# Cross-attention on one core: running sums of a pair's projection in PSUM tiles of their own, and two pieces of GpSimd's work moved

## The chip, the cores and the metric

One core of one Trainium2 chip runs the kernel. The metric is the device time of one execution in microseconds (us), from runs that are repeated; the profile is of one more execution. TensorE (PE) does the matrix products, with its weight loads in rows of their own (PEld); VectorE (DVE), ScalarE (ACT) and GpSimd (POOL) do the elementwise work; SyncE (SP) issues most transfers. Products land in PSUM, which TensorE writes and VectorE and ScalarE read.

## What is computed

Sixteen batch elements, each with 100 tokens of width 640 (`x`) and 722 context rows of width 384, eight heads of width 80. The last 4 context rows (`ca`) are apart from the first 718 (`enc`). Cut to what matters:

```python
query = x @ Wq
hs = mha(query, enc @ Wk, enc @ Wv)
ca_q1 = einsum('btc,th->bch', ca, Wq_ca)[:, indices, :]
ca_hs1 = mha(ca_q1, x, x)                      # first stage of the tokens
ca_hs2 = mha(ca_hs1 @ Wq, ca @ Wk_ca, ca @ Wv_ca)
out = (hs + ca_hs2) @ Wout + b_out + x
```

All of it is float32. `mha` is softmax attention over eight heads.

## The kernel before, in words

**Order of the work.** After a set-up, a loop over the 16 batch elements b issues everything in an order written out by hand: `tc.manual_schedule` keeps each engine's instructions in the order in which the program calls them. The framework only adds the waits between engines. An instruction that must wait therefore holds up all that stands behind it on its engine.

**One batch element.** TensorE computes the scores of b (`scores`, L650, in three groups, two of them in two-bank PSUM tiles and one in single banks), then the small products of the tokens' stages (L851, L789), then the values of b and the keys of b + 1 (`Values`, L475, and `Keys`, L506), both from sums of blocks that save products; the last third of the keys (`last_keys`, L600); in odd b the queries of the next two elements (`queries`, L576); then, in some b, the projection of two row tiles of the output (below); then the softmax's row sums (L1540) and the weighted values (L1558). ScalarE and VectorE move results out of PSUM between these; VectorE finds and subtracts maxima (L1382, L713 to L743, L1370), ScalarE takes exponentials (L1378).

**PSUM.** There are eight banks in three pools: `ps2` with two tiles of two banks each (`pair`), `psk` with two single banks (`psumk`) and `ps1` with two single banks (`psum1`). Each pool hands out its buffers in turn, so a tile can be written only when the last reader of the tile two allocations before it in its pool is done. `Keys` A and B and one score group use `psk`; `Values` A and B, the other scores and the last keys use `ps2`; `queries` alternate between `psk` and `ps1`.

**Projection in pairs.** The output's 1600 rows are cut into row tiles r of 128 rows (the last three apart). `ENDS[r]` is the batch element in which tile r's last row lies. Tiles 0 to 9 are projected two at a time (`project_pair`, L1104 to L1168) with a scheme that needs seven products of half-width blocks where a plain one needs eight: the sums of row blocks come from GpSimd (`row_sums`, L1102), those of weights stand ready. Four PSUM banks take part. y is a running sum: a product is added to it, VectorE adds it into the output tile, the next product is added on top, and so on, four times. z is a running sum read twice, v and w are each read once. Before, y and z are the two banks of one `ps2` tile (named `o_ps` in the profile), v and w are single banks (`o_psv`, `o_psw`). The ten tiles make five pairs, in the loop passes b = 3, 6, 8, 11 and 13. In b = 6 and 8 the helper `step` slips VectorE's steps of the next element's first-stage maximum between the adds. The end of the method sets rows of `most`, in which the row sums of the pair were kept, back on GpSimd (L1167).

**Residual and bias.** The output tile `xn` of a row tile is loaded from `x` (`Last.load`, L995, two buffers), GpSimd adds the bias (`add_bias`, L1005), and the projection is added in place (`add` in `project_pair`, L1138). `O_AFTER[r]` says with which element's `Last` this is done; the loop pass is one later. Before, it is one element earlier for the even tile of a pair (passes 2, 5, 7, 10 and 12) than for the odd one. SyncE issues the stores of a finished pair (`store`), the loads of x and the load of the tokens' matrix m (`load_m`) behind VectorE's last running maximum of the scores, in this order.

**GpSimd's queue in a pass** (b from 1 to 13): the first stage's scores of b + 1 (`scores1`, L824, L831); the tokens' keys of b + 2 (`keys`, five small products, L761, read by the next pass's L789); the second stage's probabilities (`softmax3`, L890), for which VectorE has taken sums; then, behind VectorE's second subtraction, `place` (L1067, L1070), the row sums, the bias, `values2` (L927, L931), the memset and the next context's block sums (`enc_sums`, L541). VectorE transposes the probabilities (`spread2`, L900) and stands waiting for them; behind that transpose on its queue are PSUM adds and the subtractions.

Of the kernel before, what the change touches and what calls it, by code (L numbers as in the profile page):

```python
# [14 lines left out]
B, S, H = 16, 100, 640  # L15
# [20 lines left out]
ENDS = [(lo + n - 1) // S for lo, n in OC]  # L36
# [1 line left out]


NPAIRS = 5  # L40
O_AFTER = [ENDS[r | 1] - (r + 1) % 2 for r in range(2 * NPAIRS)] + ENDS[2 * NPAIRS :]
PAIRED = {ENDS[r + 1]: (r, r + 1) for r in range(0, 2 * NPAIRS, 2)}
HT = NH * T

# [114 lines left out]
def kernel(  # L159
# [33 lines left out]
    def pair(name):  # L193
        tile = ps2.tile([P, 2, 512], F32, tag="ps2", name=name)
        return tile
# [4 lines left out]
    def psumk(name):  # L200
        return psk.tile([P, 512], F32, tag="psk", name=name)
# [543 lines left out]
    def load_m(b, behind=None):  # L745
        if b < 2:
            return lambda c: m_sb[c][:, b * HT : (b + 1) * HT]
        mb = small.tile([P, HC, HT], F32, tag="mb", name=f"mb_{b}")
        loaded = nc.sync.dma_start(
            out=mb, in_=m_d[:, :, b * HT : (b + 1) * HT].rearrange("c p n -> p c n")  # L750
        )
        if behind:
            wait_for(loaded, behind)
        return lambda c: mb[:, c]

    def keys(m):

        for c, (_, groups) in enumerate(GROUPS):
            at = [i for i, h in enumerate(groups) if h >= 0]
            n, step = len(at), at[1] - at[0]  # L760
            nc.gpsimd.tensor_tensor(  # L761
                m2[:, c, at[0] : at[-1] + 1 : step, :],
                m(c).unsqueeze(1).to_broadcast([P, n, HT]),
                hmask[:, c, :n].unsqueeze(2).to_broadcast([P, n, HT]),
                ALU.mult,
            )
# [210 lines left out]
    class Last:  # L977
# [6 lines left out]
        def load(self, behind=None):  # L984

            self.xn = {}
            for r, (lo, n) in enumerate(OC):
                if self.b != O_AFTER[r]:
                    continue
# [114 lines left out]
        def project_pair(self, steps):  # L1104

            r0, r1 = PAIRED[self.b]
            t0, t1 = hsTs[r0], hsTs[r1]
            x0, x1 = (xns[r].rearrange("p (k d) -> p k d", k=2) for r in (r0, r1))
            b11, t3 = w_there[0]
            b21, b22 = w_there[1]  # L1110
            tt1, tt2, tt4 = (wout_t[:, i] for i in range(3))
            both = pair(f"o_ps_{r0}")
            y, z = both[:, 0], both[:, 1]
            v, w = psumk(f"o_psv_{r0}"), psumk(f"o_psw_{r0}")

            def product(bank, rows, weights, first=False, last=False):
                for c in range(2):
                    nc.tensor.matmul(  # L1118
                        bank[:, : H // 2],
                        rows[:, c],  # L1120
                        weights[:, c],
                        start=(first and c == 0),
                        stop=(last and c == 1),
                        skip_group_check=True,
                    )

            def rest(bank, rows, k, last=True):
                nc.tensor.matmul(
                    bank[:, : H // 2],
                    rows[:, HC - 1],  # L1130
                    wout_sb[:, HC - 1, k * (H // 2) : (k + 1) * (H // 2)],
                    start=False,
                    stop=last,
                    skip_group_check=True,
                )

            def add(to, left):
                nc.vector.tensor_tensor(to, left, to, ALU.add)  # L1138

            def step(n=1):  # L1140
                if steps:
                    steps(n)

            step()
            product(y, t0[:, :2], b11, True)
            product(z, t1[:, :2], t3, True)
            add(x0[:, 0], y[:, : H // 2])
            step()
            product(y, self.s2, tt2)
            add(x1, both[:, :, : H // 2])  # L1150
            step()
            product(v, t0[:, 2:4], b21, True)
            rest(v, t0, 0)
            product(y, self.s1, tt1)
            add(x0[:, 1], y[:, : H // 2])
            step()
            product(z, t1[:, 2:4], tt4)
            rest(z, t1, 0)
            add(x1[:, 0], z[:, : H // 2])
            step(8)  # L1160
            product(w, self.s4, b22, True)
            rest(w, t0, 1)
            rest(y, t1, 1)
            add(x0[:, 0], v[:, : H // 2])
            add(x0[:, 1], w[:, : H // 2])
            add(x1[:, 1], y[:, : H // 2])
            nc.gpsimd.memset(most[96:, :], LOW)  # L1167
            held.extend((r, xns[r]) for r in (r0, r1))  # L1168
# [183 lines left out]
    for b in range(B):  # L1352
# [24 lines left out]
        def exponential(i):  # L1377
            nc.scalar.activation(st[i], st[i], AF.Exp, scale=SCALE)  # L1378
# [28 lines left out]
        if b == 0:  # L1407
            second.scores1()
            m_next = load_m(b + 2)
            kk.go(3)  # L1410
            top.go(3)
            first_values(3, e_in, (act, act), get=bank)
            top.go(1)
            first_values(0, e_in, (act, act), (0, 1), bank)
            second_next, enc_next = loads()
            enc_next = load_rest(b + 2, enc_next)
            now.scores2()
            kk.go(2)
            top.go()
            kk.go(3)  # L1420
            now.softmax3()
            kk.go(3)
            now.spread2()
            subtract(0)
            exponential(0)
            kk.go(2)
            subtract(1)
            kk.go(3)
            exponential(1)
            subtract(2)  # L1430
            exponential(2)
            last_keys(b + 1, enc)
            keys(m_next)
            enc_sums(enc_next)
            now.values2()
        elif b + 1 < B:
            vv = Values(b, e_in)

            def both(n):
                vv.go(n)  # L1440
                kk.go(n)

            second.scores1(seen)
            store(seen)
            last.load(seen)
            if b == B - 2:
                again()
            if b + 2 < B:
                m_next = load_m(b + 2, seen)
                keys(m_next)  # L1450
            if b == 1:
                load_outputs(nc.sync.dma_start, wout_sb, wout)
            top.go(3)
            both(3)
            now.scores2()
            top.go(1)
            both(2)
            top.go()
            both(2)
            now.softmax3()  # L1460
            both(1)
            now.spread2()
            vv.go(2)
            kk.go(1)
            subtract(0)
            exponential(0)
            vv.go(1)
            last.place(subtract(1))
            if last.b in PAIRED:
                last.row_sums()  # L1470
            last.add_bias()
            now.values2()
            vv.go(1)
            kk.go(2)
            exponential(1)
            vv.go(1)
            kk.go(2)
            both(1)
            both(1)
            if b == 1:  # L1480
                for f in list(wv_there):
                    nc.scalar.copy(wv_sb[:, W_AT[f]], wv_there.pop(f))
            if b == 1:
                nc.gpsimd.dma_start(out=bias, in_=bout[0].partition_broadcast(P))
            second_next, enc_next = loads()
            subtract(2)
            exponential(2)
            last_keys(b + 1, enc)
            if b + 2 < B:
                enc_next = load_rest(b + 2, enc_next)  # L1490
        else:
            vv = Values(b, e_in)
            last.place()
            last.load()
            mine.load()
            last.add_bias(seen)
            top.go(3)
            vv.go(3)
            last.project_few(len(OC) - 2)
            last.project((0,), True, put=False)  # L1500
            top.go(1)
            now.scores2()
            top.go()
            now.softmax3()
            less = subtract(0)
            now.spread2()
            exponential(0)
            wait_for(subtract(2, nc.gpsimd), less)
            now.values2()
            mine.add_bias()  # L1510
            vv.go(5)
            last.put()
            vv.go(1)
            subtract(1)
            exponential(2)
            vv.go(1)
            exponential(1)
            vv.go(5)
# [109 lines left out]
```

## Time and profile before

| | |
|---|---|
| median of 3 runs | 939.08 us (938.87 to 940.33) |
| the profiled execution's own time | 939.93 us |
| its span | 938.2 us |
| instructions | 26084 |
| granted TensorE clock | full in all 40 slices |
| transferred | 69.50 MB, mean 74 GB/s |
| busiest engine after TensorE | VectorE, 660.2 us |

The profile is of one execution. The span runs from its first to its last instruction; what lies around it is the difference to its own time. Rows of a timeline give the start within the span, the duration, engine, line, operation, output and inputs, the shape, how many instructions are put together, and in brackets the idle time of the engine just before them with what ended it. A float32 product of 128 rows is two matmul instructions in the trace for each one in the program. Rows of waits give total, number and longest.

### The profile page before, as it was taken

What the parts mean: (1) busy time and instruction counts of PE and PEld (TensorE: products, weight loads), DVE (VectorE), ACT (ScalarE), POOL (GpSimd) and SP (SyncE); (2) the same over time, 40 slices, a digit from 0 to 9 for tenths busy, and PEclk for the clock granted to TensorE, in tenths of its full rate; (3) what the DMA queues carried; (4) which work ended last, traced back from release to release, by engine and by line L of the source; (5) the groups of instructions that cost most, each with busy time, mean ns of one, the idle gap of its engine ahead of it and who ended that gap; (6) DMA issues with size and microseconds to landing.
All of it is one profiled execution on the core that took longest, in us unless ns stands there. A gap on an engine that the chain in (4) does not pass through costs nothing.

```text
span 938.2 us, 26084 instructions
## 1 busy us (share of the span) xinstructions
PE 921.5 (98%) x11163; PEld 777.7 (83%) x11163; DVE 660.2 (70%) x1116; ACT 374.8 (40%) x649; POOL 611.8 (65%) x646
## 2 busy tenths in 40 slices
PE   9999999999999999999999999999999999999998
PEld 6997879797887979878798787988887888878865
DVE  3358895979739796675957759578792887828784
ACT  1234544444325443432434334344541444414451
POOL 5848857587746868475684746756974578745553
PEclk9999999999999999999999999999999999999999
DMA  8613352050401403140231402204140150401312
GB/s 260 201 45 101 62 120 65 19 140 19 107 12 47 126 21 107 29 129 12 68 88 29 129 12 73 76 21 131 28 108 10 48 137 22 108 11 45 79 50 70
DMA packets 68956, 69.50 MB, mean 74 GB/s; under 512 B 26088, under 2 KB 62632, under 8 KB 68840
## 3 DMA queue, kind: packets, MB, share of 16 engines
q1 hardware_dynamic: 67512, 66.51, 26.8%
q8 instruction: 88, 1.44, 0.7%
q10 hardware_dynamic: 864, 0.98, 0.4%
q0 software_dynamic: 464, 0.34, 0.2%
q14 instruction: 28, 0.23, 0.1%
HBM read 62.14 MB, written 8.94 MB: 76 GB/s over the span
## 4 chain that ended last, share of the span: by engine, by line
PE 91%; DVE 6%; ACT 1%; issue 1%; POOL 0%; DVEq 0%; POOLq 0%; ACTq 0%
PE s_ps L650 12%; PE v_psA L475 10%; PE v_psB L475 8%; PE kT_ps L600 8%; PE a_ps L1558 7%; PE q_ps L576 7%; PE k_psA L506 7%; PE k_psB L506 6%; PE r_ps L1540 4%; PE v_psC L475 3%; PE o_ps L1118 3%; PE k_psC L506 3%; PE y_ps L789 2%; PE v_ps L416 2%; DVE most L1382 2%; PE v_psD L475 1%
## 5 line engine op out<-in xcount | busy, mean ns | idle before, releaser
L824 POOL TENSOR_TENSOR e<-ca,g 100x800 f32<-100x800 f32 x64 | 99.2, 1560 | 105.7 <-DVE most L1382 90.4
L541 POOL TENSOR_TENSOR enc<-enc 128x240 f32<-128x240 f32 x135 | 109.8, 823 | 19.7 <-ACT qp L584 10.1
L475 PE MATMUL v_psA<-wv_sb,enc 128*120 128x320 f32 x352 | 109.6, 434 | 0.4 <-ACT st L678 0.3
L650 PE MATMUL s_ps<-qp,kT 32*120 32x100 f32 x3072 | 97.7, 263 | 0.0
L650 PEld LDWEIGHTS s_ps<-qp,kT 32*120 32x120 f32 x3072 | 94.9, 179 | 2.1 <-issue 0.2
L831 POOL TENSOR_TENSOR e<-e,e 100x800 f32<-100x800 f32 x48 | 90.3, 1882 | 3.8
L475 PE MATMUL v_psB<-wv_sb,enc 128*120 128x320 f32 x296 | 91.8, 433 | 0.0
L506 PE MATMUL k_psA<-enc,wk_sb 128*128 128x240 f32 x360 | 87.8, 367 | 0.6 <-DVE kT L446 0.5
L1370 DVE TENSOR_TENSOR st<-st,over 120x1600 f32<-120x1600 f32 x47 | 86.2, 1834 | 0.0
L1382 DVE TENSOR_TENSOR most<-most,st 120x800 f32<-120x800 f32 x64 | 69.6, 1088 | 21.8 <-ACT st L672 20.7
L506 PEld LDWEIGHTS k_psA<-enc,wk_sb 128*128 128x128 f32 x360 | 68.2, 190 | 17.7 <-DVE kT L446 0.9
L475 PEld LDWEIGHTS v_psA<-wv_sb,enc 128*120 128x120 f32 x352 | 63.2, 183 | 23.2 <-DVE vs L446 1.0
L1378 ACT ACTIVATE st<-st 120x1600 f32<-120x1600 f32 x48 | 73.9, 1540 | 9.1 <-DVE st L1370 8.8
L1393 DVE TENSOR_TENSOR most<-st 120x800 f32<-120x800 f32 x16 | 18.6, 1160 | 81.6 <-ACT st L678 81.6
L506 PE MATMUL k_psB<-enc,wk_sb 128*128 128x240 f32 x300 | 73.1, 366 | 0.1
L475 PEld LDWEIGHTS v_psB<-wv_sb,enc 128*120 128x120 f32 x296 | 54.1, 183 | 21.9 <-DVE vs L446 0.4
L1067 POOL TENSOR_TENSOR hsT<-hsT,ratio 128x500 f32<-128x500 f32 (+22 forms) x26 | 20.5, 789 | 78.3 <-DVE st L1370 73.5
L1558 PE MATMUL a_ps<-st,vs 120*64 120x100 f32 (+1 forms) x1536 | 69.5, 250 | 0.0
L576 PE MATMUL q_ps<-xT,wq_sb 128*128 128x200 f32 x400 | 69.1, 333 | 0.0
L1558 PEld LDWEIGHTS a_ps<-st,vs 120*64 120x64 f32 (+1 forms) x1536 | 66.4, 137 | 2.7 <-issue 2.7
L576 PEld LDWEIGHTS q_ps<-xT,wq_sb 128*128 128x128 f32 x400 | 67.9, 190 | 0.2
L678 ACT COPY st<-s_ps 120x800 f32<-120x800 f32 x64 | 49.7, 829 | 43.9 <-PE s_ps L650 43.9
(193 smaller groups left out, 1906.7 us busy)
## 6 DMA issues: line engine op xcount, KB each, us to landing
pb<-p_d SPq DMA_DIRECT2D x32, 400.0 KB
enc<-in_enct SPq DMA_DIRECT2D x30, 240.0 KB
enc<-in_enct SPq DMA_DIRECT2D x15, 360.0 KB
xT<-in_xt SPq DMA_DIRECT2D x8, 500.0 KB
rest<-in_enct SPq DMA_DIRECT2D x31, 120.0 KB
xn<-in_x SPq DMA_DIRECT2D x11, 320.0 KB
wide_d<-p_d SPq DMA_DIRECT2D x16, 200.0 KB
pb<-wide_d SPq DMA_DIRECT2D x16, 200.0 KB
```

The costliest lines, as they stand in the source:

```text
L475: nc.tensor.matmul(at[0][j][:KN, : H // 2], a_form(self.enc, f)[:, j * KN : (j + 1) * KN], wv_there.get(f, wv_sb[:, W_AT[f]]), start=first ...
L506: nc.tensor.matmul(at[:, i * KT : (i + 1) * KT], wk_sb[:, W_AT[f], i], a_form(self.enc, f), start=(first and i == 0), stop=last, skip_grou ...
L541: nc.gpsimd.tensor_tensor(out, left, right, op)
L576: nc.tensor.matmul(q_ps[:, : 2 * S].rearrange("p (j s) -> p j s", j=2), wq_sb[:, c, n * P : (n + 1) * P], xT[:, :, c, :], start=(c == 0), ...
L600: nc.tensor.matmul(bank[:, i * KT : (i + 1) * KT], weights[c], a_raw(enc, u, c), start=(i == 0 and c == 0), stop=(c == CC - 1), skip_group ...
L650: nc.tensor.matmul(s_ps[bank][:n, 256 * a + lo : 256 * a + lo + rhs.shape[-1]], kT[rows, c, u, j * KN : (j + 1) * KN], rhs, start=bank not ...
L824: first = nc.gpsimd.tensor_tensor(to, self.ca[:, t, :].unsqueeze(1).to_broadcast([S, NH, S]), g[:, :, t].unsqueeze(2).to_broadcast([S, NH, ...
L831: nc.gpsimd.tensor_tensor(e, e, to, ALU.add)
L1370: return engine.tensor_tensor(st[i], st[i], top.over[:KN].unsqueeze(1).to_broadcast([KN, 2, ROWS]), ALU.subtract,)
L1378: nc.scalar.activation(st[i], st[i], AF.Exp, scale=SCALE)
L1382: most_now = nc.vector.tensor_tensor(most[:KN], most[:KN], st[i][:, u], ALU.max)
L1558: nc.tensor.matmul(wides[64 * e : 64 * e + 64, h // 2], slot(i, h, FIRST[e], 64), st[i // 2][: KEYS[i], i % 2, h * S : (h + 1) * S], start ...
```

## The change

Three edits, of which the first two touch the projected pairs and the third every pass from 1 to 13:

- y and z become two single-bank tiles (`o_psy`, `o_psz`) and v and w the two banks of one `ps2` tile (`o_ps`). The add that read y and z in one instruction is split in two; the adds of v and w become one.
- `O_AFTER` of the even tile of a pair becomes that of the odd one: both residual tiles are loaded and get their bias in the pair's own pass.
- `keys` for b + 2 is called behind `softmax3`, not ahead of it; its load stays where it was.

```diff
-O_AFTER = [ENDS[r | 1] - (r + 1) % 2 for r in range(2 * NPAIRS)] + ENDS[2 * NPAIRS :]
+O_AFTER = [ENDS[r | 1] for r in range(2 * NPAIRS)] + ENDS[2 * NPAIRS :]
...
+            y, z = psumk(f"o_psy_{r0}"), psumk(f"o_psz_{r0}")
             both = pair(f"o_ps_{r0}")
-            y, z = both[:, 0], both[:, 1]
-            v, w = psumk(f"o_psv_{r0}"), psumk(f"o_psw_{r0}")
+            v, w = both[:, 0], both[:, 1]
...
             product(y, self.s2, tt2)
-            add(x1, both[:, :, : H // 2])
+            add(x1[:, 0], y[:, : H // 2])
+            add(x1[:, 1], z[:, : H // 2])
...
-            add(x0[:, 0], v[:, : H // 2])
-            add(x0[:, 1], w[:, : H // 2])
+            add(x0, both[:, :, : H // 2])
             add(x1[:, 1], y[:, : H // 2])
...
                 m_next = load_m(b + 2, seen)
-                keys(m_next)
...
             now.softmax3()
+            if b + 2 < B:
+                keys(m_next)
             both(1)
             now.spread2()
```

## The prediction, made before the run

> **What bounds the kernel now.** I read the page's busy times and chain first, then the waits of TensorE alone, then the timeline around a pair's projection.
>
> From the page of before, the busy row of every engine and the chain that ended last:
>
> ```profile
> PE 921.5 (98%) x11163; PEld 777.7 (83%) x11163; DVE 660.2 (70%) x1116; ACT 374.8 (40%) x649; POOL 611.8 (65%) x646
> ...
> PE 91%; DVE 6%; ACT 1%; issue 1%; POOL 0%; DVEq 0%; POOLq 0%; ACTq 0%
> ```
>
> TensorE is busy 921.5 us of a span of 938.2, so it idles 938.2 - 921.5 = 16.7 us. No edit that leaves its matmuls alone can win more than about that, and only edits that touch those idle times win anything. Who causes them (columns: us in total, times, longest):
>
> ```profile
> PE o_ps L1118 <- DVE xn L1138: 6.7, 10, 0.8
> PE k_psE L506 <- DVE vs L446: 1.5, 3, 0.8
> PE z_ps L851 <- issue: 1.4, 2, 0.9
> ```
>
> The first row is the pair projection: ten waits, two in each of five pairs, all for VectorE's adds out of PSUM. It is the largest single wait of the engine that bounds the kernel. One pair in full, batch 3 (start, us, engine, line, out, count, wait in brackets), TensorE and then VectorE:
>
> ```profile
> 255.24 2.32 PE L1118 MATMUL o_ps<-wout_sb,hsT 128*128 128x320 f32 x8
> 258.23 1.31 PE L1118 MATMUL o_ps<-wout_t,most 128*128 128x320 f32 x4 [0.68 <-DVE xn L1138]
> 259.38 1.24 PE L1118 MATMUL o_psv<-wout_sb,hsT 128*128 128x320 f32 x4
> 260.46 0.70 PE L1128 MATMUL o_psv<-wout_sb,hsT 128*128 128x320 f32 x2
> 261.00 1.24 PE L1118 MATMUL o_ps<-wout_t,most 128*128 128x320 f32 x4
> 262.82 1.34 PE L1118 MATMUL o_ps<-wout_t,hsT 128*128 128x320 f32 x4 [0.58 <-DVE xn L1138]
> ...
> 266.16 0.70 PE L1128 MATMUL o_ps<-wout_sb,hsT 128*128 128x320 f32 x2
> ```
>
> ```profile
> 257.60 0.49 DVE L1138 TENSOR_TENSOR xn<-o_ps,xn 128x320 f32<-128x320 f32 x1 [5.60 <-PE o_ps L1118]
> 259.66 0.83 DVE L1138 TENSOR_TENSOR xn<-o_ps,xn 128x640 f32<-128x640 f32 x1 [1.57 <-PE o_ps L1118]
> 262.28 0.49 DVE L1138 TENSOR_TENSOR xn<-o_ps,xn 128x320 f32<-128x320 f32 x1 [1.80 <-PE o_ps L1118]
> ```
>
> The eight matmuls at 255.24 are y's four and z's four. The first add needs y alone, yet begins at 257.60, just behind the end of both (255.24 + 2.32 = 257.56). At 262.82 TensorE wants z and waits for the add at 262.28, which reads y. So y and z, two banks of one tile, are guarded as one thing. That is what the change takes apart.
>
> **The change part by part.**
>
> *Size of what goes.* From 259.38 to 261.00 six matmuls are issued without a wait: 1.62 / 6 = 0.27 us each. From 255.24 to 266.16 there are 34 starts, so 34 x 0.27 = 9.18 us undisturbed against 10.92: the pair loses 1.74 us, of which the brackets show 0.68 + 0.58 = 1.26. The rest, 0.48, is the array emptying before each wait and refilling behind it. Over five pairs: 6.7 from the wait row, plus 5 x 0.48 = 2.4, is **9.1 us**.
>
> *What is late next, first wait.* Take y's start as zero. y ends at 1.24 (the length of four matmuls, as at 259.38); VectorE's add can run from 1.28 to 1.77 (0.04 behind the end, as 257.60 behind 257.56; then 0.49). TensorE resumed 0.14 behind the add (258.23 behind 258.09), so y is free again at 1.91. Meanwhile z's four matmuls keep TensorE until 8 x 0.27 = 2.16. Slack 0.25 us: the wait is covered. The slack is thin. Were the wait just touched, the pair would pay the refill behind it, which four matmuls show as 1.31 against 1.24: I bound what stays at 0 to 0.1 us a pair, and take 0, since the slack is over three times that.
>
> *Second wait.* The next y product starts at 2.16 and ends at 3.40; its add runs from 3.44 to 3.93. TensorE has v's six matmuls from 3.24 to 4.86 before it needs y. Slack 0.8. z then needs only the add of its own bank, which comes from 3.93 to 4.42, and z is wanted at 5.94. In batches 6 and 8 VectorE also works through a maximum between these adds. Batch 6 now:
>
> ```profile
> 421.28 0.98 DVE L715 TENSOR_REDUCE quad<-turned 128x25 f32<-128x800 f32 x1
> 422.93 0.82 DVE L1138 TENSOR_TENSOR xn<-o_ps,xn 128x640 f32<-128x640 f32 x1 [0.68 <-PE o_ps L1118]
> 423.67 0.70 DVE L718 TENSOR_REDUCE side<-quad 32x25 f32<-32x25 f32 x4
> 424.41 1.31 DVE L725 TENSOR_REDUCE mx<-side 32x25 f32<-32x100 f32 x4
> 425.75 0.49 DVE L1138 TENSOR_TENSOR xn<-o_ps,xn 128x320 f32<-128x320 f32 x1
> 426.30 1.34 PE L1118 MATMUL o_ps<-wout_t,hsT 128*128 128x320 f32 x4 [0.78 <-DVE xn L1138]
> ```
>
> The 0.98 us reduction would end near 1.77 + 0.98 = 2.75, ahead of 3.44; the 2.0 us group delays only the third add, whose bank y isn't written again until the last product. So both batches lose their waits too.
>
> *Adds.* One add of 0.83 becomes two of 0.49, and two of 0.49 become one of 0.83: 0.3 us more, then less, on an engine with 278 us idle. Cost 0.
>
> *Where the new tiles wait at their start.* y and z now take the two single-bank buffers that query projections or the next keys had; v and w take the two-bank buffer later than y and z did, so they have more room. In batches 3 and 11 z takes the buffer of the query product before the last, which is copied out a whole product earlier; in 6 and 8 y and z take those of the next keys, with the last third of those keys still ahead of the pair on TensorE. In batch 13 z takes the buffer of the last query product, which ScalarE empties in
>
> ```profile
> 822.48 0.74 ACT L588 ACTIVATE qz<-q_ps,qmask 128x200 f32<-128x200 f32 x2 [1.37 <-PE q_ps L576]
> ```
>
> that is until 823.22, where y starts at 822.28 in before and z is due 1.08 later, at 823.36. A wait of 0 to 0.1 us, once. I take 0.
>
> *Tokens' keys behind the probabilities, 13 batches.* GpSimd and VectorE in batch 3:
>
> ```profile
> 229.86 1.40 POOL L761 TENSOR_TENSOR m<-mb,hmask 128x64 f32<-128x64 f32 x5
> 231.22 0.23 POOL L890 TENSOR_TENSOR p_in<-e,sm 100x32 f32<-100x32 f32 x1
> 236.47 0.78 POOL L1067 TENSOR_TENSOR hsT<-hsT,ratio 128x280 f32<-128x280 f32 x1 [5.02 <-DVE st L1370]
> ```
>
> ```profile
> 231.49 0.21 DVE L900 STREAM_TRANSPOSE p2t<-p_in 128x32 f32<-128x32 f32 x1 [0.17 <-POOL p_in L890]
> 231.63 1.78 DVE L1370 TENSOR_TENSOR st<-st,over 120x1600 f32<-120x1600 f32 x1
> ...
> 242.03 2.10 DVE L1370 TENSOR_TENSOR st<-st,over 120x1600 f32<-120x1600 f32 x1
> ```
>
> The five keys' products (1.40 us) move into the 5.02 us in which GpSimd waits anyway, and the transpose no longer waits 0.17. It stands before VectorE's subtractions and PSUM adds, so up to 13 x 0.17 = 2.2 us come off VectorE's queue. TensorE has no wait row behind that place, so the gain is 0, at most some tenths. The keys are read only by the next batch's first-stage product. What they may cost: they now touch VectorE's subtraction. The row at 242.03 took 2.10 us beside GpSimd's bias add, 1.78 to 1.81 elsewhere, so 0.3 us a batch at most, 13 x 0.3 = 3.9 us of VectorE in the worst case. The Trainium skill ("SBUF — State Buffer", section "Who interferes with whom") speaks against the move: a VectorE instruction with two SBUF inputs contends with a GpSimd instruction that reads SBUF. The trace agrees with it in the 2.10. By that rule the sum would lose those 0.3 us a batch only if TensorE waited for VectorE there; by the rows it doesn't, and the sum stays.
>
> *The even tile's load and bias, one batch later.* In each pair's batch SyncE issues two loads of x, and GpSimd adds two biases. Batch 6:
>
> ```profile
> 414.13 3.14 POOL L1005 TENSOR_TENSOR xn<-xn,bias 128x640 f32<-128x640 f32 x1
> L1005 POOL TENSOR_TENSOR xn<-xn,bias x13: 858/1544/3137, 191.2 to 901.9; 128x640 f32<-128x640 f32 x11, 64x320 f32<-64x320 f32 x2
> 429.38 0.76 POOL L1167 MEMSET most<- 32x800 f32 x1 [4.21 <-PE o_psw L1118]
> ```
>
> The second bias runs from 417.27 and takes 1.54 (the median) to 3.14: done by 418.8 to 420.4. The pair starts at 418.52, and the add that needs this tile is due 3.44 later, at 421.96: slack 1.6 to 3.1 us. Behind it on GpSimd stand values2 and the memset, which idles 4.21 us; the wait for w comes 1.9 earlier, so 2.3 of it is left, against 1.54 to 3.14. At the worst the row sums of the next context start as late as now. In batches 2, 5, 7, 10 and 12 GpSimd is freed by the same amount. The load itself: slices of 0.35 us from 386 us on, in which the issues at 388.9 (320 KB of x, 80 KB of m) run:
>
> ```profile
> GB/s 0 0 0 0 0 0 0 0 0 0 0 110 102 358 348 211 41 0 0 0 0 0 0 0 0 0 0 0 0 0 0 0 23 0 0 0 0 0 0 47
> ```
>
> All has landed by 392. A second 320 KB adds 1 to 1.5 us, some 20 us ahead of 414. The m load behind it has until the keys. Cost 0.
>
> *Sum.* -9.1 us (bounds: 5 x 0.1 + 0.1 = 0.6 for what may stay of the waits; -0.5 for VectorE's earlier transposes, an estimate). The profiled execution took 939.93 us, 1.73 more than its span; it would become 930.8. Its time lies 0.85 above the median of the three runs, 939.08, and against this median the forecast is 939.08 - 9.1 = **930.0 us**.
>
> **The rivals.**
>
> 1. *Half is given back.* TensorE reaches the next batch 1.8 us earlier and may meet an engine that isn't ready, or the first, thin cover fails and only the second wait goes (5 x 0.9 = 4.5). For: the 0.25 us slack. Against: behind scores, VectorE and GpSimd wait for TensorE's results, as the 4.21 us shows. About 934.6 us.
>
> 2. *The waits stay.* If the guards count TensorE's matmuls in order and the first add still goes behind z, nothing moves. For: the add at 257.60 starts with z's end, which fits either reading. Against: 262.82 waits for an add that read y only, which order on TensorE doesn't explain. 939 us.
>
> 3. *Slower: the second bias comes too late.* VectorE's add into the odd tile waits for it, y's next product for the add, TensorE for both. GpSimd's place is 1.6 us of slack (batch 6, at 3.14 us); from there each us costs five, and beyond 1.6 + 1.8 = 3.4 us late the kernel is slower. Five us late would be (5 - 1.6) x 5 - 9.1 = +7.9: 947 us. Against: the transfers are done 20 us before, and GpSimd's queue up to the second bias holds only what it held.
>
> **How the numbers follow.** A measurement can tell about 0.2%, 1.9 us, from no change. Full gain, 929.0 to 931.0: 0.72. More, down to 928.4, if earlier transposes also spare k_psE's 1.5 us: 0.05. Rival 1, 931 to 936: 0.13. Rival 2, within 0.2%: 0.06. Rival 3: 0.04. So faster 0.90, same 0.06, slower 0.04. The range 928.8 to 932.6 holds the full gain, most of the case below it and the near part of rival 1, about 0.8.
>
> **What would show it.** Right: the ten waits of the o_ps row gone or under 0.1 us each; the first add of a pair beginning about 1.3 us behind the pair's first matmul, not 2.36; from the pair's first matmul to the start of its last two, 9.2 us instead of 10.9; the p_in wait of the transpose gone, the k_psE row as it was. Wrong: a wait of TensorE for the new z at its first product; VectorE's add waiting for a bias; a longer subtraction with a TensorE wait behind it; or the pairs shorter by 1.8 us each and the batches between them longer by as much.

## The result, and the profile after

The changed kernel takes 931.04 us (median of 4 runs, 929.79 to 932.29) where the kernel before took 939.37 in the same measurement: ratio 0.991, 95% interval 0.9893 to 0.9927. Measured once more beside other kernels it took 930.76 against 940.05. The forecast was 930.0. The profiled execution took 930.72 us with a span of 929.0, so the span shrank by 938.2 - 929.0 = 9.2 us; the sum had said 9.1.

The page after, busy times and chain:

```profile
PE 918.7 (99%) x11163; PEld 778.2 (84%) x11163; DVE 669.6 (72%) x1116; ACT 374.9 (40%) x649; POOL 611.1 (66%) x646
...
PE 94%; DVE 4%; issue 1%; ACT 1%; DMA 0%; POOL 0%; SPq 0%; DVEq 0%; ACTq 0%
```

TensorE's idle time fell from 16.7 us to 929.0 - 918.7 = 10.3, which is 6.4 of the 9.2; the other 2.8 came off its busy time (921.5 to 918.7). VectorE's part of the chain fell from 6% to 4%. Of VectorE's 9.4 us more of busy time, 4.7 are the subtractions that the change lengthens (below). Copies in the set-up (L1293 and L1301) took 14.0 us in this execution where they took 3.5 before, which is not the change's doing: a second profile of the changed kernel has 3.5 again. The longest waits of TensorE after the change:

```profile
PE k_psE L506 <- DVE vs L446: 1.6, 4, 0.7
PE idle_ps L1224 <- DVE vaT L1221: 1.1, 1, 1.1
PE z_ps L851 <- issue: 0.9, 2, 0.5
```

The row with the ten waits for the pair's adds, 6.7 us, is gone; k_psE, which the change doesn't touch, stands first. The pair of batch 3 in the timeline of TensorE and of VectorE:

```profile
255.72 1.24 PE L1118 MATMUL o_psy<-wout_sb,hsT 128*128 128x320 f32 x4
256.79 1.24 PE L1118 MATMUL o_psz<-wout_sb,hsT 128*128 128x320 f32 x4
257.87 1.24 PE L1118 MATMUL o_psy<-wout_t,most 128*128 128x320 f32 x4
258.94 1.24 PE L1118 MATMUL o_ps<-wout_sb,hsT 128*128 128x320 f32 x4
...
260.56 1.24 PE L1118 MATMUL o_psy<-wout_t,most 128*128 128x320 f32 x4
261.64 1.24 PE L1118 MATMUL o_psz<-wout_t,hsT 128*128 128x320 f32 x4
...
264.87 0.70 PE L1128 MATMUL o_psy<-wout_sb,hsT 128*128 128x320 f32 x2
```

```profile
257.06 0.49 DVE L1138 TENSOR_TENSOR xn<-o_psy,xn 128x320 f32<-128x320 f32 x1 [5.33 <-PE o_psy L1118]
259.22 0.49 DVE L1138 TENSOR_TENSOR xn<-o_psy,xn 128x320 f32<-128x320 f32 x1 [1.66 <-PE o_psy L1118]
259.62 0.48 DVE L1138 TENSOR_TENSOR xn<-o_psz,xn 128x320 f32<-128x320 f32 x1
261.84 0.49 DVE L1138 TENSOR_TENSOR xn<-o_psy,xn 128x320 f32<-128x320 f32 x1 [1.73 <-PE o_psy L1118]
```

No row of TensorE has a bracket: groups of four follow each other at 1.07 to 1.08 us. From the first start to the start of the last two it is 264.87 - 255.72 = 9.15 us, where it was 10.92. VectorE's first add starts 1.34 behind the pair's first matmul, while z's product runs, not 2.36 behind it, at z's end.

### The profile page after: what moved, and what is told of

Same layout as the page of the kernel before. It is cut to its first block, busy times and chain, and to the rows that moved or that the text cites. A ratio compares the mean times of both kernels' runs of the same rounds, so it can differ in the third digit from the quotient of the medians.

```text
span 929.0 us, 26080 instructions
## 1 busy us (share of the span) xinstructions
PE 918.7 (99%) x11163; PEld 778.2 (84%) x11163; DVE 669.6 (72%) x1116; ACT 374.9 (40%) x649; POOL 611.1 (66%) x646
## 4 chain that ended last, share of the span: by engine, by line
PE 94%; DVE 4%; issue 1%; ACT 1%; DMA 0%; POOL 0%; SPq 0%; DVEq 0%; ACTq 0%
PE s_ps L650 12%; PE v_psA L475 10%; PE v_psB L475 8%; PE kT_ps L600 7%; PE a_ps L1559 7%; PE q_ps L576 7%; PE k_psA L506 7%; PE k_psB L506 6%; PE r_ps L1541 4%; PE v_psC L475 3%; PE k_psC L506 3%; PE v_ps L416 2%; PE y_ps L789 2%; PE o_psy L1118 2%; PE v_psD L475 2%; PE v_psE L475 1%
## 5 line engine op out<-in xcount | busy, mean ns | idle before, releaser
L1370 DVE TENSOR_TENSOR st<-st,over 120x1600 f32<-120x1600 f32 x47 | 90.9, 1934 | 0.0
```

What stands on the lines that cost most here:

```text
L1370: return engine.tensor_tensor(st[i], st[i], top.over[:KN].unsqueeze(1).to_broadcast([KN, 2, ROWS]), ALU.subtract,)
```

## The experiments

**One part alone.** The first kernel has only the PSUM edit of the diff on the kernel before, the second only the two moves:

```diff
+            y, z = psumk(f"o_psy_{r0}"), psumk(f"o_psz_{r0}")
             both = pair(f"o_ps_{r0}")
-            y, z = both[:, 0], both[:, 1]
-            v, w = psumk(f"o_psv_{r0}"), psumk(f"o_psw_{r0}")
+            v, w = both[:, 0], both[:, 1]
...
-            add(x1, both[:, :, : H // 2])
+            add(x1[:, 0], y[:, : H // 2])
+            add(x1[:, 1], z[:, : H // 2])
...
-            add(x0[:, 0], v[:, : H // 2])
-            add(x0[:, 1], w[:, : H // 2])
+            add(x0, both[:, :, : H // 2])
```

```diff
-O_AFTER = [ENDS[r | 1] - (r + 1) % 2 for r in range(2 * NPAIRS)] + ENDS[2 * NPAIRS :]
+O_AFTER = [ENDS[r | 1] for r in range(2 * NPAIRS)] + ENDS[2 * NPAIRS :]
...
                 m_next = load_m(b + 2, seen)
-                keys(m_next)
...
             now.softmax3()
+            if b + 2 < B:
+                keys(m_next)
```

> The kernel before with y and z as tiles of their own, the keys and the even tile's load and bias where they were. My theory (VectorE's guard goes by the tile, so z's and v's products now cover the adds): the whole gain, 8 to 9.5 us under the kernel before; 9.15 us from a pair's first matmul to the start of its last two, no o_ps wait on TensorE; the transpose's waits for p_in (2.2 us in 12) stay. Rival (the gain is the moves': GpSimd's queue and the earlier transposes): within 2 us of the kernel before.

> The kernel before with only the keys and the even tile's load and bias moved; y and z share a tile. My theory: within 1 us of the kernel before, ten o_ps waits of 6.7 us in all as there, p_in waits of the transpose gone, VectorE's subtractions some 4 to 5 us longer in sum (the page after has 90.9 against 86.2) with no wait of TensorE behind them. Rival (the moves bring the gain): 5 to 9 us faster.

> The changed kernel once more, on the chip of the other runs. My theory: equal to the kernel with only the PSUM edit within 1 us, 8 to 9.5 us under the kernel before. Rival (the moves cost or bring something of their own through the longer subtractions or the spared waits): more than 1.5 us away from the kernel with only the PSUM edit.

Measured on one chip, beside 940.05 us of the kernel before: the PSUM edit alone 930.73 us (ratio 0.9904, interval 0.9889 to 0.9919), the moves alone 939.57 (0.9999, 0.999 to 1.0007), the whole change 930.76 (0.9903, 0.9889 to 0.9916). The PSUM edit is all of the gain, and the two moves together are worth nothing that shows, within 1 us either way. They were not run apart from each other. The waits of TensorE with the moves alone, first row, and those of VectorE with the PSUM edit alone:

```profile
PE o_ps L1118 <- DVE xn L1138: 6.5, 10, 0.8
```

```profile
DVE p2t L900 <- POOL p_in L890: 2.2, 12, 0.2
```

The moves leave the ten waits as they were; without them the transpose still waits 2.2 us for the probabilities, and the kernel is as fast. With them, in the changed kernel, that wait is gone.

**How thin is the cover of the first wait?** The changed kernel, with the first add of a pair cut into four adds of a quarter of y each, so that the last ends later:

```diff
-            add(x0[:, 0], y[:, : H // 2])
+            for _ in range(4):
+                nc.vector.scalar_tensor_tensor(
+                    x0[:, 0], y[:, : H // 2], 0.25, x0[:, 0], ALU.mult, ALU.add
+                )
```

> The changed kernel with the first add of each pair done as four adds of a quarter of y each (the same sum). Each add starts 0.40 us behind the one before, so the last ends 1.2 us later. My slack reckoning (y free 0.14 us behind the add, 0.25 us of slack): y's second product starts 3.1 us behind the pair's first matmul where it was 2.15, with a wait of some 0.8 us in the row; a pair takes 10.1 to 10.2 us, in all about 5 us over the changed kernel, 936. Rival (the cover is larger than I think, since TensorE was not waiting for that add at all): below 932.5.

Measured: 937.54 us, 6.8 over the changed kernel on the same chip, and not the 5 expected. TensorE and VectorE in batch 3:

```profile
257.05 1.24 PE L1118 MATMUL o_psy<-wout_sb,hsT 128*128 128x320 f32 x4
258.13 1.24 PE L1118 MATMUL o_psz<-wout_sb,hsT 128*128 128x320 f32 x4
260.62 1.31 PE L1118 MATMUL o_psy<-wout_t,most 128*128 128x320 f32 x4 [1.25 <-DVE xn L1148]
```

```profile
258.40 2.07 DVE L1148 SCALAR_TENSOR_TENSOR xn<-o_psy,xn 128x320 f32<-128x320 f32 x4 [5.34 <-PE o_psy L1118]
```

The four adds take 2.07 us, 0.52 each: each starts behind the end of the one before (one alone takes 0.49), where I had let them follow at 0.40 like the two adds at 259.22 and 259.62 above. Those two write different halves of a row tile; these four each read what the one before wrote. That this is the reason is likely, but no run shows it. The first starts 1.35 behind the pair's first matmul, and TensorE resumes 260.62 - 260.47 = 0.15 behind the last. So in the changed kernel y is free at 1.34 + 0.49 + 0.15 = 1.98 where its next product is due at 2.15: the slack is 0.17 us, not 0.25. By this reckoning an add longer by a third of its time would bring the wait back. That the added 1.58 us cost 3.57 - 2.15 = 1.42 of start is the same 0.16 by another way.

**Does the guard go by the tile?** The same products with other neighbours: z and v share the two-bank tile, w is single.

```diff
-            y, z = psumk(f"o_psy_{r0}"), psumk(f"o_psz_{r0}")
+            y, w = psumk(f"o_psy_{r0}"), psumk(f"o_psw_{r0}")
             both = pair(f"o_ps_{r0}")
-            v, w = both[:, 0], both[:, 1]
+            z, v = both[:, 0], both[:, 1]
```

> The changed kernel with the banks shared out otherwise: y and w single banks, z and v the two banks of one tile; the adds of v and w are apart again. Theory (the guard goes by the tile): v's first product must wait for the add that reads z; 1.3 us of wait in each pair, a pair 10.5 us, in all some 7 us over the changed kernel, 937 to 939. Rival (the guard goes by the bank, or by the order of TensorE's products, and the gain came from elsewhere in the rearrangement): no wait at v, 930 to 932.

Measured: 937.05 us (ratio to the kernel before 0.9971, 0.9962 to 0.998), 6.3 over the changed kernel's 930.76. This run and those below were made on another chip than that 930.76; the kernel before took 939.84 to 940.01 us beside them, and 940.05 there. The waits of TensorE, then TensorE and VectorE in batch 3:

```profile
PE o_ps L1118 <- DVE xn L1138: 5.2, 5, 1.1
```

```profile
257.17 1.24 PE L1118 MATMUL o_psy<-wout_t,most 128*128 128x320 f32 x4
259.46 1.34 PE L1118 MATMUL o_ps<-wout_sb,hsT 128*128 128x320 f32 x4 [1.05 <-DVE xn L1138]
```

```profile
258.93 0.48 DVE L1138 TENSOR_TENSOR xn<-o_ps,xn 128x320 f32<-128x320 f32 x1
```

TensorE waits with v's first product until the add that reads z, another bank, is over (258.93 + 0.48 = 259.41). The row shows 1.05 us of wait where 1.3 was expected; the pair takes 10.47 us from its first start to that of its last two, 1.32 more than the changed kernel's and as expected. The rival, a guard by banks or by the order of products, has no reason for this wait. It is the mechanism of the kernel before, put at another place.

**The late bias.** The rival that would have been slower, made to happen: the biases stand behind `values2` on GpSimd.

```diff
-            last.add_bias()
             now.values2()
+            last.add_bias()
```

> The changed kernel with GpSimd's biases behind values2 in each pass, which puts them some 8 us later. It tries my rival of the late bias. Slack reckoning: in passes 6 and 8, where no queries stand before the pair, the first tile's bias ends near 422 where the add is due at 418.4: TensorE waits some 3.5 us in each, 7 us in all; in 3, 11 and 13 the biases are done 1 us or more before the pair: nothing. 936 to 939 us, with waits of VectorE's xn for GpSimd. Rival (GpSimd has more room than I reckon): within 1.5 us of the changed kernel.

Measured: 946.22 us (ratio 1.0075, 1.0056 to 1.0093), slower than the kernel before, and 15.5 over the changed one where 5 to 8 were expected. The place was right: in passes 3, 11 and 13 the pair is undisturbed, in 6 and 8 VectorE waits for the bias and TensorE for VectorE, 9.8 us in two waits. The size was not: a wait is 4.88 us where 3.5 was reckoned, and the rest of the loss follows the waits. Pass 6, VectorE, TensorE, and the busy times by stretch (the columns: length; busy us and instructions of PE, PEld, DVE, ACT, POOL; granted TensorE clock; share and rate of transfers):

```profile
422.78 0.49 DVE L1138 TENSOR_TENSOR xn<-o_psy,xn 128x320 f32<-128x320 f32 x1 [8.40 <-POOL xn L1005]
```

```profile
423.32 2.50 PE L1118 MATMUL o_psy<-wout_t,most 128*128 128x320 f32 x4 [4.88 <-DVE xn L1138]
```

```profile
412.00:417.00 5.00, 5.00 (x26) 4.50 (x25) 2.38 (x2) 3.34 (x5) 4.53 (x4) 1.00 0.71 214
418.50:423.00 4.50, 0.00 (x0) 0.00 (x0) 0.22 (x1) 0.00 (x0) 4.42 (x5) 0.99 0.00 0
423.00:426.00 3.00, 2.68 (x5) 1.85 (x6) 1.23 (x3) 0.00 (x0) 1.24 (x1) 0.50 0.00 0
426.00:429.00 3.00, 3.00 (x12) 2.06 (x11) 2.78 (x11) 0.00 (x0) 0.00 (x0) 0.94 0.00 0
```

Four matmuls behind the wait take 2.50 us in place of 1.24, at a granted clock of 0.50. In pass 6 the pair lasts 15.79 us and in pass 8 17.28, against 9.15: 14.8 us in all, of which 9.8 are the waits.

**How long must a wait be for the clock to fall?** The first add cut into eight, as before into four:

> The changed kernel with the first add of each pair done as eight adds of an eighth of y. From the run with four: 0.52 us an add, the first 1.34 us behind the pair's first matmul, TensorE 0.15 behind the last: y's second product 5.65 us behind the pair's first matmul, a wait of 3.3 us in the row where four adds gave 1.25. If a wait costs its own length and a refill, whatever its length: 5 x 3.6 = 18 us over the changed kernel, 949. If the granted clock falls for some us behind a wait of this length, as it did behind 4.9 us in the run with the late biases (0.50 in the stretch behind it): 2 to 5 us more in some or all pairs, 952 to 970, and a granted clock under 1.00 in those stretches.

Measured: 954.04 us (1.015, 1.0133 to 1.0168), 23.3 over the changed kernel, where the waits alone would give 18. TensorE in batches 3 and 6, and two stretches behind the wait of batch 3:

```profile
261.29 2.47 PE L1118 MATMUL o_psy<-wout_t,most 128*128 128x320 f32 x4 [3.35 <-DVE xn L1148]
263.56 2.34 PE L1118 MATMUL o_ps<-wout_sb,hsT 128*128 128x320 f32 x4
...
429.23 1.31 PE L1118 MATMUL o_psy<-wout_t,most 128*128 128x320 f32 x4 [3.35 <-DVE xn L1148]
430.38 1.24 PE L1118 MATMUL o_ps<-wout_sb,hsT 128*128 128x320 f32 x4
```

```profile
262.00:265.00 3.00, 3.00 (x7) 1.98 (x6) 0.89 (x2) 0.00 (x0) 0.00 (x0) 0.50 0.00 0
268.00:271.00 3.00, 3.00 (x13) 2.13 (x12) 0.98 (x2) 0.00 (x0) 0.00 (x0) 1.00 0.00 0
```

Behind the same wait of 3.35 us the clock is halved in batch 3 and not in batch 6. In four of the five pairs some matmuls run at half rate, which makes these pairs 1.6 to 3.0 us longer than batch 6's 12.74; the waits of the five are 3.35, 3.35, 3.34, 3.35 and 3.25 us. Behind the 1.25 us of the run with four adds none do.

**The next wait in the row.** With the pair's waits gone, k_psE stands first: the keys' block E needs the single banks that VectorE empties of the values' block E, and ahead of that on VectorE stands the 1.0 us transpose that spreads the scores' maximum. One place later for that transpose:

```diff
             both(2)
+            vv.go(1)
             top.go()
-            both(2)
+            vv.go(1)
+            kk.go(2)
             now.softmax3()
```

> The changed kernel with VectorE's spreading transpose of the scores' maximum (1.0 us) one place later, behind the adds of the value blocks E, so that the single banks of the keys' block E come free sooner. Reckoning from the changed kernel: the k_psE waits of TensorE (1.6 us in 4, on its weight loads 3.7) go, 1 to 3 us faster, 928 to 930. Rival (the transpose then holds up the next adds and TensorE waits there, or the waits were the refill of another bound): within 1 us.

> The changed kernel with the later transpose of the maximum, again, on the chip of the two others: 927 to 929 us if its gain of some 2.8 us over the changed kernel is real; 930 to 931 if it was the chip.

> The kernel before with only the PSUM edit and the later transpose of the maximum; keys, load and bias where they were. If the moves are worth nothing, it equals the run of the changed kernel with that transpose later, within 1 us: 927 to 929. If the moves' longer subtractions (4.7 us of VectorE in sum) begin to count once the k_psE waits are gone, it is 1 to 2 us faster than that run; if the spared waits of the transpose of the probabilities count, as much slower.

Measured: 927.95 us (0.9876, 0.9861 to 0.9891), again 928.57 (0.9876, 0.9859 to 0.9894), and without the moves 928.97 (0.9883, 0.9866 to 0.9901). All three beat the kernel before. Over the changed kernel the gain is 2.2 to 2.8 us, by its 930.76; it was not measured beside them, and its ratio to the kernel before, 0.9903 (0.9889 to 0.9916), has an interval that overlaps theirs at the edge, so the size is less sure than the sign. The moves are worth nothing here too: the two kernels that were measured side by side, 928.57 and 928.97, differ by less than can be told. VectorE in pass 5, after the change and with the transpose later:

```profile
340.00 1.00 DVE L743 STREAM_TRANSPOSE over<-spread 128x800 f32<-128x800 f32 x1
340.93 0.85 DVE L446 TENSOR_TENSOR vs<-v_psE,vs 120x320 f32<-120x320 f32 x2
```

```profile
338.74 0.88 DVE L446 TENSOR_TENSOR vs<-v_psE,vs 120x320 f32<-120x320 f32 x2
339.54 1.00 DVE L743 STREAM_TRANSPOSE over<-spread 128x800 f32<-128x800 f32 x1
```

No k_psE row is left among TensorE's waits in any of the three profiles. The last pass of this kernel shows one new wait of TensorE, 1.0 us for VectorE's adds of values in the first of the two runs, which the second doesn't have among its longest.

## Why the prediction was right, by its steps

- *The size of what goes*, 9.1 us from 6.7 of waits and 2.4 of emptying and refilling: the span fell by 9.2, the medians by 8.3 in the first measurement and by 9.3 in the second. The 2.4 lay in time that the profile counts as busy, which fell by 2.8; so the prediction's opening, that only TensorE's idle 16.7 us can be won, was too narrow, and its sum was right to count more than idle time. Had the wait row alone been taken, a quarter of the gain would have been missed.
- *The guard by the tile*: shown by putting z beside v, which brings a wait of 1.05 us in batch 3 and 5.2 us of waits in the five pairs. It is also what sets Rival 2's order reading aside.
- *Slack of the first wait*: 0.25 was too much. The add starts 0.10 behind y's end, not 0.04, and TensorE resumes 0.15 behind it: 0.17. The step held, since nothing crossed it.
- *The second wait, batches 6 and 8, the adds*: the five pairs have no wait. *The new z in batch 13* costs its pair 0.09 us (9.24 against 9.15; z's four matmuls take 1.31), inside the 0 to 0.1: z starts at 815.96, 0.14 behind the end of ScalarE's copy.
- *Keys behind the probabilities*: the gain of 0 held, and so did the reason. What VectorE pays was put at 3.9 us "in the worst case", and it is all of that and more. The subtractions before and after:

```profile
L1370 DVE TENSOR_TENSOR st<-st,over 120x1600 f32<-120x1600 f32 x47 | 86.2, 1834 | 0.0
```

```profile
L1370 DVE TENSOR_TENSOR st<-st,over 120x1600 f32<-120x1600 f32 x47 | 90.9, 1934 | 0.0
```

  That is 4.7 us more in 13 passes, 0.36 each: the first subtraction now takes 2.13 us beside the keys, where it took 1.78. With the PSUM edit alone the sum is 86.2 again. The term was under-sized, and it cost nothing, because no wait of TensorE hangs on that subtraction. The Trainium skill ("SBUF — State Buffer", section "Who interferes with whom") has the two contend, and the trace agrees; that the change lost nothing by it is a matter of what stands behind, as the prediction's rows had said.
- *The even tile's load and bias*: two biases in a row take 4.64 us, that is 3.14 and 1.5, and the pair of pass 6 finds them done:

```profile
412.70 4.64 POOL L1005 TENSOR_TENSOR xn<-xn,bias 128x640 f32<-128x640 f32 x2
```

  They end at 417.34, and the first add that needs the second tile is due 3.44 behind the pair's start at 417.09.
- *The rivals*: nothing was given back (the intervals between the pairs' starts shrank by 1.74 to 2.48 us), and the waits did not stay. The slower rival is a true mechanism that the change doesn't reach, but its price was wrong twice: two passes pay, not five, as in the odd ones the queries stand ahead of the pair; and behind a long wait comes the slower clock, which I had not counted.

## What to carry to other kernels

Where the bounding engine waits a little, often, for another to read what it wrote, look at what is guarded together: here two banks in one tile waited for each other's readers, and a tile of its own lets the neighbour's products cover the turnaround. Reckon the gain from start to start, not from the idle times, and reckon the slack of what covers it, for it may be 0.2 us. A move on an engine off the path is worth nothing until a row of the bounding engine names it, even if it shortens or lengthens that other engine's work by microseconds.

## What the runs showed of the hardware that was not expected

Waits of TensorE of 3.25 to 3.35 us were followed in four of five cases by 3 to 6 us at about half the clock, waits of 4.88 us in both of two, and waits of 1.15 to 1.25 us in none of five. The one wait of 3.35 us without the slower clock cost its pair its own length and 0.24 us (12.74 - 9.15 - 3.35); the six with it cost 1.5 to 3.0 us beyond that. Waits between 1.25 and 3.25 us were not tried. The Trainium skill ("TensorE: Matmul & The Clock Gate", section "HAM oscillation — how this bites in real kernels") warns of TensorE idle gaps above about 3.4 us, after which the clock is halved. The trace agrees in the clock of 0.50; its border lies near that figure but is not sharp, as four of five waits a little under it were followed by the slower clock and one was not.
